# Turning the weights of a three-layer field-interaction kernel: W1 and W0 in one transfer each, V2 spread over interleaved rows, and a new order of TensorE's first products

## The chip, the core and the metric

The kernel runs on one core of one Trainium2 chip. The metric is the device time in microseconds (us). The median of three runs of the kernel before is 738.91 us (738.64 to 738.91).

## The reference, cut to what matters

```python
def _cin_layer(Xk, X0, W, b):                # X0: [B, F, E] = [1024, 39, 64]
    Wr = W.reshape(O, Hk, F)                 # O = H = 64
    return jnp.einsum('bhe,bfe,ohf->boe', Xk, X0, Wr) + b[None, :, None]

Xk = X0
for W, b in ((W0, b0), (W1, b1), (W2, b2)):  # W0: 64 x 39*39, W1 and W2: 64 x 64*39
    Xk = _cin_layer(Xk, X0, W, b)
    outs.append(Xk.sum(axis=-1))
y = jnp.concatenate(outs, axis=-1) @ fc_w.T + fc_b
```

All of it is linear in each weight, so the kernel folds the last layers together. With fc2 the third part of `fc_w`, V2[h, f] is the sum over o of fc2[o] W2[o, h, f]. With V2 (and fc1 as its fortieth column), T[h, f, b] is the sum over o of V2[o, b] W1[o, h, f]. For every sample and every e, the output is then the dot product of two vectors of 64 quadratic forms in the 39 field values: one with the weights W0, one with the weights T plus fc0. Small terms for the biases are added at the end.

## The kernel before, in words

**The main loop.** The 1024 samples times 64 give 65536 columns, taken in 32 blocks of 2048. GpSimd gathers copies of the field rows into tiles `r` (five per block, `gather_rows`, L170; lists of rows in `lists`) and, for each two blocks, `u` and `v`. VectorE multiplies pairs of tiles into products `p` (L211, L213): six chunks of 128 field pairs per block, and one small chunk of 32 rows for each two blocks. TensorE multiplies each `p` with the weights `wa` (L538, L558, L569) into four banks `po`; ScalarE and VectorE finish a block into `sums`. Products are made four steps ahead of TensorE (`AHEAD = 4`).

**The preparation (L216 to L491), where the change lies.** It makes `both`: 64 rows with W0 and 64 rows with T, each with 39 x 40 columns. From `both`, VectorE and ScalarE add the two halves of each field pair into `pairs` (`weight_rows`, L505 and L503), TensorE turns `pairs` (L522), and ScalarE copies it to `wa` (L523, L524). The schedule is written by hand: each engine runs its instructions in the order of the code. The steps on TensorE, with `spin` (L277) a product of constants whose result nobody reads:

1. one `spin` of 512 columns; then `fc_w` turned into columns of the bank `small` (L322, L320), then a `spin` of 512;
2. V2: four products of W2 (`w2s`, 128 rows) with `fc2`, which VectorE makes from `small` (L366), into two banks `pv` (L404). VectorE transposes the banks in 32 x 32 squares (L427), and VectorE and ScalarE copy the columns into two diagonal blocks of `v2` (L437, L438), with fc1 beside them (L434);
3. W0 turned by 20 transposes (L415) from `w0s`, which two transfers have filled on 39 rows each;
4. a `spin` of 512; the biases turned from `brow` (L320, called at L422 and L424); a `spin` of 256;
5. T: four products of W1 (`w1s`, two transfers of 64 rows) with `v2` (L457), copied to `part` (L468), turned by 20 transposes (L477) and copied into `both` (L486). W0 is copied into `both` at L453.
6. two `spin`s of 512, which reach to the first turn of `pairs`.

**The queues.** ScalarE issues the transfers of W2, the first half of the first block's x (`xh[0]`), W0 (two), W1 (two) and `xh[1]`, in this order, before its first computing instruction. SyncE issues `fc_w`, the biases, and then the two copies `xd<-xh` (L394). GpSimd makes small constants (L313, L354 to L358; `pairs` is zeroed at L356), sends a row of ones to DRAM (L361), gathers four `r` from `xh[0]`, loads the second block's x, and gathers four `r` from `xh[1]`, then `r`, `u` and `v` from `xd`.

Of the kernel before, what the change touches and what calls it, by code (L numbers as in the profile page):

```python
# [54 lines left out]
F32 = mybir.dt.float32  # L55
I32 = mybir.dt.int32
AF = mybir.ActivationFunctionType
ALU = mybir.AluOpType
AX = mybir.AxisListType

B, F, E, H = 1024, 39, 64, 64
FH = F * H
FT = F + 1
# [3 lines left out]
NT = 5  # L67
# [7 lines left out]
NCHUNK = NPAIR + 2  # L75
MM = 512
# [3 lines left out]
NQ = NA // 2  # L80
NW = 20
BB = BLK // E
# [4 lines left out]
U_STEPS = ((10, -29), (20, -8), (23, -2), (25, -36), (28, 32))  # L87
V_STEPS = ((0, -3), (20, 6), (25, 33), (28, -35), (31, -39))
# [56 lines left out]
def cin_kernel(ctx: ExitStack, tc: tile.TileContext, x, w0t, b0, w1, b1, w2, b2, fc_w, fc_b, out):  # L145
    nc = tc.nc
# [3 lines left out]
    const = ctx.enter_context(tc.tile_pool(name="const", bufs=1))  # L150
# [6 lines left out]
    xd = [dram.tile([2 * FT, BLK], F32, name=f"xd{k}") for k in range(NTAB)]  # L157
# [17 lines left out]
    def roll(n, tiles=range(NT)):  # L175
        for i in tiles:
            k = n % 2 * NT + i
            gather_rows(rt[n % 2][:, i], xd[n // 2 % NTAB][: FT if k < NT else 2 * FT], k)

    def roll_small(n):  # L180
        table = xd[n // 2 % NTAB].rearrange("f (t c) -> (f t) c", c=SUB)
        for k, dst in enumerate((ut, vt)):
            gather_rows(dst[n // 2 % 2], table, 2 * NT + k)

    wa = const.tile([128, NCHUNK, 3 * H], F32, name="wa")
    columns = const.tile([128, 7], F32, name="columns")
    v2 = const.tile([128, 2, H], F32, name="v2")
    fc0s, b0s = columns[:, 1:2], columns[:, 3:4]
    fcb = const.tile([1, 1], F32, name="fcb")
# [3 lines left out]
    lists = const.tile([128, 2 * NT + 2], I32, name="lists")  # L193
# [23 lines left out]
    with prep as prep:  # L217
        w2s = prep.tile([128, FH // 2], F32, name="w2s")
        w1s = prep.tile([128, FH // 2], F32, name="w1s")
        w0s = prep.tile([128, NW * H], F32, name="w0s")  # L220
        part = prep.tile([FT, 4 * NA, H], F32, name="part")
        fcrow = prep.tile([1, 3 * H], F32, name="fcrow")
        brow = prep.tile([1, 3 * H], F32, name="brow")
        fcrow2 = prep.tile([1, H, 2], F32, name="fcrow2")
        fc2 = prep.tile([128, H], F32, name="fc2")
# [15 lines left out]
        nc.vector.memset(warm, 0.0)  # L241
        w0v = w0t.rearrange("b a h -> b (a h)")
        nc.sync.dma_start(fcrow, fc_w)
        for k, t in enumerate((b0, b1, b2)):
            nc.sync.dma_start(brow[:, k * H : k * H + H], t.rearrange("(o h) -> o h", o=1))
        nc.scalar.dma_start(w2s, w2.rearrange("o (s n) -> (o s) n", s=2))

        def load_half(k):
# [4 lines left out]
        load_half(0)  # L253
        for s, n in enumerate((NW, F - NW)):
            nc.scalar.dma_start(
                w0s[H * s : H * s + F, 0 : n * H], w0v[:, s * NW * H : (s * NW + n) * H]
            )
        for s in range(2):
            nc.scalar.dma_start(
                w1s[H * s : H * s + H], w1[:, s * FH // 2 : (s + 1) * FH // 2]  # L260
            )
        load_half(1)
        nc.gpsimd.iota(place, pattern=[[0, 1]], base=0, channel_multiplier=1)
        nc.gpsimd.iota(apart, pattern=[[1, 128]], base=0, channel_multiplier=-1)
        nc.scalar.copy(warm, warm)


# [7 lines left out]
        def spin(n=1, cols=MM // 2):  # L275
            for _ in range(n):
                nc.tensor.matmul(  # L277
                    idle[:, 0:cols],
                    nc.const_aps.tensor(1.0, (128, 128), F32),
                    nc.const_aps.tensor(1.0, (128, cols), F32),  # L280
                    start=True,
                    stop=True,
                )

        spin(1, MM)

# [23 lines left out]
        for i in range(NT):  # L310
            at = OFFSET[i] - 3 * K + (0 if i < NT - 1 else -F)
            for k, by in enumerate((STEP[i], BASE[i], at)):
                nc.gpsimd.memset(shifts[:, k, i : i + 1], float(by))  # L313
        for s in range(2):
            nc.gpsimd.tensor_copy(fcrow2[:, :, s], fcrow[:, 2 * H : 3 * H])
        one = ones[0:1, 0, 0:1]

        def turn_row(h, at, row, k):
            dst = small[h : h + H, at : at + 1]
            nc.tensor.matmul(dst, row[:, k * H : k * H + H], one, start=True, stop=True)  # L320

        nc.tensor.matmul(  # L322
            small[:, 0:1], fcrow2.rearrange("p h s -> p (h s)"), one, start=True, stop=True
        )
        for k, at in enumerate((1, 2, 4)):
            turn_row(0, at, fcrow, k)
        for k in range(2):
            turn_row(H, k + 1, fcrow, k)
        spin(1, MM)

# [20 lines left out]

        for k, series in enumerate((U_STEPS, V_STEPS)):
            for i, (at, by) in enumerate(series):
                nc.gpsimd.memset(steps_at[:, k, i : i + 1], float(at))  # L354
                nc.gpsimd.memset(steps_by[:, k, i : i + 1], float(by))
        nc.gpsimd.memset(pairs, 0.0)  # L356
        bothv = both.rearrange("p (a b) -> p a b", b=FT)
        nc.gpsimd.memset(bothv[0:H, :, F], 0.0)  # L358

        def fill_ones(k, engine, src):  # L360
            engine.dma_start(xd[k][F::FT].rearrange("r (p c) -> p r c", c=128), src)  # L361

        fill_ones(0, nc.gpsimd, ones)


        nc.vector.tensor_scalar(fc2[:, 0::32], mask, small[:, 0:1], None, ALU.mult)  # L366
        nc.vector.tensor_scalar(unit, apart, 0, None, ALU.is_equal)

# [12 lines left out]
        fused(most, r, 4.0, most, ALU.add, ALU.add)  # L381
        nc.vector.tensor_tensor(seat, seat, far, ALU.add)
        nc.vector.tensor_tensor(both_of[:, 0:1], most, jumps[:, 0:1], ALU.add)
        nc.vector.tensor_tensor(both_of[:, 1:2], both_of[:, 0:1], jumps[:, 1:2], ALU.add)
        nc.vector.tensor_scalar(lists[:, 2 * NT :], both_of, 2.0, seat, ALU.mult, ALU.add)

        halves = [slice(0, SUB), slice(SUB, BLK)]
        for k, cols in enumerate(halves):
            for i in range(4):
                gather_rows(rt[0][:, i, cols], xh[k], i)  # L390
            if not k:
                load(1, nc.gpsimd)
        for k, cols in enumerate(halves):
            nc.sync.dma_start(xd[0][0:F, cols], xh[k])  # L394
        roll(0, (4,))
# [15 lines left out]

        for s in range(2):
            for k in range(NW // 2):
                n = min(128, (F - NW * s) * H - k * 128)
                nc.tensor.transpose(  # L415
                    pw[s][0:n, k * FT : k * FT + F],
                    w0s[H * s : H * s + F, k * 128 : k * 128 + n],
                    unit[H * s : H * s + F, H * s : H * s + F],
                )
        spin(1, MM)  # L420
        for h in (0, H):
            turn_row(h, 3, brow, 0)  # L422
        for k in (1, 2):
            turn_row(0, k + 4, brow, k)  # L424
        spin()
        for k in range(2):
            nc.vector.transpose(  # L427
                blocks[:, k].rearrange("p (f h) -> p f h", h=32),
                pv[k][:, 0:320].rearrange("p (h f) -> p f h", f=10),
            )  # L430
        column = blocks.rearrange("h k (f j) -> h (k f) j", j=32)[:, :, 0]
        for s in range(2):
            rows = slice(H * s, H * s + H)
            nc.scalar.copy(v2[rows, s, F:FT], small[rows, 2:3])  # L434
        for s in range(2):
            rows = slice(H * s, H * s + H)
            nc.vector.tensor_copy(v2[rows, s, 0:20], column[0:H])  # L437
            nc.scalar.copy(v2[rows, s, 20:F], column[H:128, 1:20])  # L438

        roll_small(0)  # L440
        roll(1)
        nc.sync.dma_start(fcb, fc_b.rearrange("(p o) -> p o", o=1))
        fill_ones(2, nc.gpsimd, ones)

# [3 lines left out]

        for k, (a, n) in enumerate(((0, NW), (NW, F - NW))):
            for t in range(2):  # L450
                m = (n + 1 - t) // 2
                src = pw[k][H * t : H * t + H, 0 : m * FT].rearrange("h (a b) -> h a b", b=FT)
                copies[k](bothv[0:H, a + t : a + t + 2 * m - 1 : 2, 0:F], src[:, :, 0:F])  # L453
        w1v = w1s.rearrange("o (h f) -> o h f", f=F)
# [27 lines left out]
        for k, a in groups:  # L482
            for t in range(2):
# [5 lines left out]
                )  # L489
        spin(2, MM)  # L490
        first = [prods.tile([128, BLK], F32, name="p", tag="p") for _ in range(3)]  # L491
# [125 lines left out]
    def last_weights(pk):  # L617

        fc1, fc2, b1c, b2c = (columns[0:H, at : at + 1] for at in (2, 4, 5, 6))
        nc.tensor.matmul(pk[0:F, 0:1], v2[0:H, 0, 0:F], b1c, start=True, stop=True)  # L620
        nc.tensor.matmul(pk[0:1, 1:2], b1c, fc1, start=True, stop=False)
        nc.tensor.matmul(pk[0:1, 1:2], b2c, fc2, start=False, stop=True)
        nc.vector.memset(wfin[0:H], 1.0)
        nc.scalar.copy(wfin[H : H + F], pk[0:F, 0:1])
        nc.scalar.activation(kfin, pk[0:1, 1:2], AF.Identity, bias=fcb, scale=float(E))
# [10 lines left out]
    for k, (n, c) in enumerate(steps[:3]):  # L636
# [12 lines left out]
        else:  # L649
            product(n, c, halves[0], p[n, c])  # L650
    nc.scalar.copy(columns[0:H, 1:7], small[0:H, 1:7])
    nc.scalar.copy(columns[H:128, 1:4], small[H:128, 1:4])
# [114 lines left out]
```

## Time and profile before

| | |
|---|---|
| median of the runs | 738.91 us |
| the profiled execution, and its span from first to last instruction | 738.49 us, 736.7 us |
| TensorE (PE) busy | 732.2 us, 99% of the span |
| VectorE (DVE) busy | 641.0 us, 87% |
| GpSimd (POOL) busy | 386.2 us, 52% |
| ScalarE (ACT) busy | 167.3 us, 23% |
| first main product (L538) starts | 22.10 us after the span's start |

Times below are us after the span's start. "PEld" is TensorE's loading of weights, "SPq", "ACTq" and "PEq" are the engines' own queues of instructions. A product of float32 appears as two records. A busy engine is not an engine at its peak: matmuls are pipelined and their ends are modelled. In the table of groups, a row has the line, the engine, what is written from what, the count, the busy time, the mean duration of one, and the idle time before it with what ended it.

### The profile page before, as it was taken

To read this page: it belongs to the slowest core of one execution; us is meant where nothing else is said; L and a number is where in the kernel's file an instruction comes from. 1 tells how busy PE (TensorE), PEld (TensorE's weight loads), DVE (VectorE), ACT (ScalarE), POOL (GpSimd) and SP (SyncE) were. 2 spreads that over 40 slices of the span, in tenths; PEclk is the share of its full clock that TensorE was granted. 3 is DMA by queue.
4 is the path that set the end of the run, shared out by engine and by line. 5 is a ranking of instruction groups with operands and counts; after the bars stand their busy time and mean duration, and the time that the engine had idled before them with its cause. 6 is when DMAs were issued, how large, how long until landed. Compare 5 with 4: busy or idle time off the path is not lost.

```text
span 736.7 us, 6437 instructions
## 1 busy us (share of the span) xinstructions
PE 732.2 (99%) x2416; PEld 318.0 (43%) x2416; DVE 641.0 (87%) x521; ACT 167.3 (23%) x244; POOL 386.2 (52%) x248
## 2 busy tenths in 40 slices
PE   9999999999999999999999999999999999999998
PEld 5444444444444444444444444444444444444443
DVE  5998899888899888899888899888899888899885
ACT  2332122221212222122221212222122221212222
POOL 6887554457545365554457545365554457545300
PEclk9999999999999999999999999999999999999999
DMA  8989867877576786757878676795767876566700
GB/s 275 376 321 414 300 237 274 347 285 274 227 285 254 286 328 248 282 226 284 334 269 279 244 283 250 287 357 215 282 240 278 328 284 247 217 259 250 285 1 1
DMA packets 65819, 197.25 MB, mean 268 GB/s; under 512 B 39987, under 2 KB 40052, under 8 KB 45819
## 3 DMA queue, kind: packets, MB, share of 16 engines
q0 software_dynamic: 28624, 185.56, 64.8%
q1 hardware_dynamic: 35472, 9.28, 5.5%
q10 hardware_dynamic: 1690, 1.99, 1.0%
q8 instruction: 19, 0.31, 0.2%
q14 instruction: 14, 0.11, 0.0%
HBM read 196.76 MB, written 10.60 MB: 281 GB/s over the span
## 4 chain that ended last, share of the span: by engine, by line
PE 98%; DVE 1%; ACT 0%; issue 0%
PE po L538 90%; PE po L558 4%; PE po L569 2%; PE idle L277 1%; DVE pairs L505 0%; PE pv L404 0%; PE pt L457 0%; DVE p L211 0%; PE pw L415 0%; PE pv L457 0%; PE small L320 0%; PE tr L522 0%; ACT part L468 0%; DVE g L588 0%; DVE sums L610 0%
## 5 line engine op out<-in xcount | busy, mean ns | idle before, releaser
L538 PE MATMUL po<-p,wa 128*128 128x512 f32 x1536 | 665.0, 593 | 0.1
L211 DVE TENSOR_TENSOR p<-r 128x2048 f32<-128x2048 f32 (+2 forms) x197 | 434.1, 2235 | 72.8 <-PE po L538 72.7
L171 POOL DMA_INDIRECT r<-xd,lists x156 | 308.6, 1978 | 286.3 <-issue 277.9
L538 PEld LDWEIGHTS po<-p,wa 128*128 128x128 f32 x1536 | 289.9, 190 | 370.5 <-issue 351.4
L586 ACT ACTIVATE z<-po,columns 64x512 f32<-64x512 f32 x128 | 87.3, 682 | 382.5 <-PE po L569 219.6
L588 DVE SCALAR_TENSOR_TENSOR g<-po,columns,z 64x512 f32<-64x512 f32 x128 | 95.9, 749 | 9.3 <-ACT z L586 5.3
L581 ACT COPY g<-r 39x1024 f32<-39x1024 f32 x64 | 66.7, 1043 | 152.1 <-DVE sums L599 124.9
L599 DVE TENSOR_REDUCE sums<-g 103x16 f32<-103x1024 f32 x62 | 75.6, 1220 | 2.1
L171 POOL DMA_INDIRECT v<-xd,lists x16 | 33.8, 2115 | 4.9 <-issue 4.9
L558 PE MATMUL po<-p,wa 32*64 32x512 f32 x512 | 31.6, 600 | 0.0
L171 POOL DMA_INDIRECT u<-xd,lists x16 | 28.4, 1772 | 4.9 <-issue 4.9
L213 DVE TENSOR_TENSOR p<-u,v 128x1024 f32<-128x1024 f32 x16 | 19.5, 1218 | 0.0
L558 PEld LDWEIGHTS po<-p,wa 32*64 32x64 f32 x512 | 9.4, 131 | 20.2 <-issue 19.4
L569 PE MATMUL po<-u,wa 32*64 32x512 f32 x256 | 17.0, 587 | 0.0
L277 PE MATMUL idle<-const-float32-1.0 128*128 128x512 f32 (+2 forms) x16 | 10.2, 752 | 0.8 <-PEq L754 0.8
L171 POOL DMA_INDIRECT r<-xh,lists x8 | 7.7, 958 | 5.2 <-issue 1.8
L569 PEld LDWEIGHTS po<-u,wa 32*64 32x64 f32 x256 | 5.7, 132 | 8.0 <-issue 8.0
L505 DVE TENSOR_TENSOR pairs<-both 128x2 f32<-128x2 f32 (+27 forms) x59 | 6.1, 171 | 0.4 <-issue 0.3
L523 ACT COPY wa<-tr 128x128 f32<-128x128 f32 x8 | 2.1, 265 | 14.8 <-PE tr L522 14.8
L468 DVE COPY part<-pt 40x320 f32<-40x320 f32 x2 | 1.0, 488 | 4.5 <-PE pt L457 4.5
L277 PEld LDWEIGHTS idle<-const-float32-1.0 128*128 128x128 f32 x16 | 3.4, 252 | 1.4 <-issue 1.2
L165 POOL DMA_DIRECT2D xd<-in_x x3 | 3.2, 1063 | 0.0
(100 smaller groups left out, 61.1 us busy)
## 6 DMA issues: line engine op xcount, KB each, us to landing
xd<-in_x SPq DMA_DIRECT2D x28, 312.0 KB
r<-xd,lists POOLq DMA_INDIRECT x156, 9.1
xd<-in_x POOLq DMA_DIRECT2D x3, 312.0 KB, 8.7
w2s<-in_w ACTq DMA_DIRECT2D x1, 624.0 KB
w1s<-in_w ACTq DMA_DIRECT2D x2, 312.0 KB
xh<-in_x ACTq DMA_DIRECT2D x2, 156.0 KB
xd<-xh SPq DMA_DIRECT2D x2, 156.0 KB
u<-xd,lists POOLq DMA_INDIRECT x16, 9.5
```

Source lines behind the costliest of these rows:

```text
L171: nc.gpsimd.indirect_dma_start(dst, None, table, bass.IndirectOffsetOnAxis(ap=lists[:, k : k + 1], axis=0))
L211: nc.vector.tensor_tensor(p[:, cols], r[:, i, cols], r[:, k, cols], ALU.mult)
L213: nc.vector.tensor_tensor(p[:, 0:SUB], ut[n // 2 % 2], vt[n // 2 % 2], ALU.mult)
L277: nc.tensor.matmul(idle[:, 0:cols], nc.const_aps.tensor(1.0, (128, 128), F32), nc.const_aps.tensor(1.0, (128, cols), F32), start=True, sto ...
L505: nc.vector.tensor_tensor(out, diagonal(a, b, sa, sb), diagonal(b, a, sb, sa), ALU.add)
L538: nc.tensor.matmul(po[n][m], wa[:, c, side : side + 2 * H], p[:, bass.ts(m, MM)], start=n % 2 == 0 and c == 0, stop=n % 2 == 1 and c == NP ...
L558: nc.tensor.matmul(dst[half * H : half * H + H], wa[rows, NPAIR, at : at + H], p[rows, bass.ts(side, MM)], start=t >= 2, stop=t < 2 and ha ...
L569: nc.tensor.matmul(dst[half : half + H], wa[rows, NPAIR + 1, H : 2 * H], ut[n // 2 % 2][rows, bass.ts(side, MM)], start=False, stop=t < 2,)
L581: nc.scalar.copy(gt[H : H + F], rt[n % 2][0:F, 0, bass.ts(m, SUB)])
L586: nc.scalar.activation(z[one], po[n][m][other], AF.Identity, bias=fc0s[other])
L588: return lambda: nc.vector.scalar_tensor_tensor(g[n][m // 2][0:H, at], po[n][m][one], b0s[one], z[one], ALU.add, ALU.mult)
L599: nc.vector.tensor_reduce(sums[:, b_at : b_at + SB], g[n][m // 2].rearrange("p (b e) -> p b e", e=E), AX.X, ALU.add,)
```

## The change

It alters how W0 and W1 lie in SBUF and in which order the preparation runs.

- W1 goes to 128 rows (row 2o + s holds half s of W1's row o) in one transfer; W0 goes to 117 rows (row 3b + s holds a third of row b) in one. `xh[0]` is issued first, W2 next.
- `v2` has a parity pattern in place of two blocks: every row 2o + s holds V2's row o in half s, and zeros in the other. The columns are spread to row pairs by two products with `twice` and multiplied with `mask`. ScalarE no longer writes `v2`.
- W0 needs 7 transposes of 117 x 128 in place of 20 of 39 x 128, and its copies into `both` change engines and pattern.
- TensorE's first `spin`s are 512 + 512 + 256 columns, and the one ahead of V2 128 in place of 512. A `spin` of 256 stands behind V2's products and another behind W0's last three turns. The biases are turned behind T.
- `pairs` is zeroed by ScalarE in place of GpSimd. SyncE's two copies `xd<-xh` change places.

```diff
-NW = 20
+NW = 3
+NF = F // NW
...
-        w0s = prep.tile([128, NW * H], F32, name="w0s")
+        w0s = prep.tile([NW * F, NF * H], F32, name="w0s")
...
-        nc.scalar.dma_start(w2s, w2.rearrange("o (s n) -> (o s) n", s=2))
         load_half(0)
-        for s, n in enumerate((NW, F - NW)):
-            nc.scalar.dma_start(
-                w0s[H * s : H * s + F, 0 : n * H], w0v[:, s * NW * H : (s * NW + n) * H]
-            )
-        for s in range(2):
-            nc.scalar.dma_start(
-                w1s[H * s : H * s + H], w1[:, s * FH // 2 : (s + 1) * FH // 2]
-            )
+        nc.scalar.dma_start(w2s, w2.rearrange("o (s n) -> (o s) n", s=2))
+        nc.scalar.dma_start(w0s, w0t.rearrange("b (s a) h -> (b s) (a h)", s=NW))
+        nc.scalar.dma_start(w1s, w1.rearrange("o (s n) -> (o s) n", s=2))
         load_half(1)
...
+        nc.scalar.copy(
+            pairs.rearrange("p c n -> p (c n)"),
+            nc.const_aps.tensor(0.0, (128, NCHUNK * 128), F32),
+        )
...
-        spin(1, MM)
+        spin(2, MM)
+        spin()
...
+        double(fcrow2, fcrow[:, H : 3 * H])
+        turn_twice(0, fcrow2, 1)
+        turn_twice(6, fcrow2, 0)
+        for h in (0, H):
+            turn_row(h, 1, fcrow, 0)
+        turn_row(0, 4, fcrow, 2)
+        spin(1, MM // 4)
...
-        nc.gpsimd.memset(pairs, 0.0)
...
+        nc.vector.tensor_scalar(unit, apart, 0, None, ALU.is_equal)
+        for h in (0, H):
+            rows = slice(h, h + H)
+            nc.vector.tensor_copy(
+                twice[rows], unit[rows, rows].unsqueeze(2).to_broadcast([H, H, 2])
+            )
         nc.vector.tensor_scalar(fc2[:, 0::32], mask, small[:, 0:1], None, ALU.mult)
+        nc.vector.tensor_scalar(v2[:, :, F], mask, small[:, 6:7], None, ALU.mult)
...
+                double(brow2, brow[:, H : 2 * H])
-        for k, cols in enumerate(halves):
-            nc.sync.dma_start(xd[0][0:F, cols], xh[k])
+        for k in (1, 0):
+            nc.sync.dma_start(xd[0][0:F, halves[k]], xh[k])
...
-        spin(1, MM)
-        for h in (0, H):
-            turn_row(h, 3, brow, 0)
-        for k in (1, 2):
-            turn_row(0, k + 4, brow, k)
         spin()
+        for k in range(4):
+            turn_w0(k)
...
+        for u, (lo, n) in enumerate(((0, 20), (1, 19))):
+            rows = slice(H * u, H * u + H)
+            nc.tensor.matmul(
+                pv[u][:, 0:n],
+                twice[rows].rearrange("p h s -> p (h s)"),
+                column[rows, lo : lo + n],
+                start=True,
+                stop=True,
+            )
+        for k in range(4, 7):
+            turn_w0(k)
+        spin()
+        for u, (lo, n) in enumerate(((0, 20), (20, 19))):
+            nc.vector.tensor_tensor(
+                v2[:, :, lo : lo + n],
+                pv[u][:, 0:n].unsqueeze(1).to_broadcast([128, 2, n]),
+                mask.unsqueeze(2).to_broadcast([128, 2, n]),
+                ALU.mult,
+            )
...
-        spin(2, MM)
+        spin(1, MM)
+        for h in (0, H):
+            turn_row(h, 2, brow, 0)
+        turn_twice(3, brow2, 0)
+        turn_row(0, 5, brow, 2)
+        spin(1, MM)
```

`turn_w0(k)` is one transpose of `w0s[:, 128k : 128k + 128]` into a quarter of a bank `pw`; `turn_twice` turns a row whose elements `double` (two copies on GpSimd) has written twice. Two list computations of VectorE move behind V2, and 20 small memsets of GpSimd ahead of `double`.

## The prediction

> **What bounds the kernel now.** I first asked where TensorE is not the limit. The busy times by stage put that aside for all but the first 42 us: in the last stage (columns: stretch, length, busy PE, PEld, DVE, ACT, POOL, granted clock, share of the DMA engines, GB/s) TensorE works 691.34 of 694.40 us.
>
> ```profile
> 42.30:736.70 694.40, 691.34 (x2275) 298.21 (x2275) 607.39 (x397) 154.11 (x196) 353.09 (x182) 1.00 0.70 264
> ```
>
> The change touches nothing there, so that stage moves as a block. What can change is when the main products begin. The chain that ended last, in order of time (start, us, what), says what sets that:
>
> ```profile
> 4.15 2.01 PE idle L277 x2
> 6.16 2.33 PE pv L404 x8
> 8.49 1.84 PE pw L415 x20
> 10.33 2.00 PE idle L277 x2
> 12.33 0.73 PE small L320 x8
> 13.06 1.15 PE idle L277 x2
> 14.21 2.22 PE pt L457 x4
> 16.43 1.57 PE pv L457 x4
> ...
> 19.61 0.37 DVE both L486
> 19.98 0.28 issue
> 20.27 0.37 DVE pairs L505 x3
> ...
> 25.41 0.30 PE tr L522
> 25.70 7.08 PE po L538 x16
> ```
>
> So the path is the queue of TensorE up to T (18.00), T's copies (to 19.98), VectorE's field pairs and first products (to 25.41), and then the main stream. T cannot start earlier because V2's last parts wait for the biases, which stand behind a dummy; the waits and the gathers' wait read
>
> ```profile
> ACT v L434 <- PE small L320: 3.9, 1, 3.9
> POOL r L171 <- DMA xh<-in_x: 1.7, 1, 1.7
> ```
>
> Last, TensorE's clock. The granted clock is given as 1.00 from the first stage on, but durations (ns min/median/max) of products of 320 columns, by tile, say that it is half until about 17 us:
>
> ```profile
> L404 PE MATMUL pv<-w2s,fc x8: 736/737/792, 6.1 to 7.7; 128*64 128x320 f32 x8
> L457 PE MATMUL pt<-w1s,v x4: 739/740/828, 14.0 to 15.7; 128*128 128x320 f32 x4
> L457 PE MATMUL pv<-w1s,v x4: 451/553/741, 16.2 to 17.5; 128*128 128x320 f32 x4
> ```
>
> **The change, part by part. TensorE at half clock.** T's first four records take 2.22 us for 4 x 320 columns, 1.7 ns a column; the main stream's 16 records take 7.08 us, 0.86 ns a column. The queue ahead of T, in the new order:
> - dummies of 512, 512 and 256 columns, two records each: 2560 x 1.7 = 4.4 us, from 0.78 to 5.2.
> - five turns of fc: 0.58 for the first 128-wide one by L322's row, 0.3 for the second behind it, six records of 0.075 (L320: 0.75 for ten): 1.2, to 6.4. Their source, doubled by GpSimd, is ready before 4 us, so the turns wait only for the dummies.
> - the dummy of 128 columns, 0.5, to 6.9. `fc2` (0.23 on VectorE) hides behind it; bare, it would cost 0.2.
> - V2, 2.33, to 9.25 (before: 8.49).
> - a dummy of 256, 1.1, to 10.35. VectorE's two square transposes (0.52 each) end beside it.
> - seven transposes. The nearest rows are 0.09 (39 x 128) and 0.3 for one alone (L522); I take 0.12: 0.8.
> - two products with `twice`, shown nowhere; four records between 0.3 (L320's rate) and 1.1 (L322's): 0.6.
> - a dummy of 256, 1.1.
>
> All at half clock, T starts at 12.85 in place of 14.21. So the new order gains 1.4 us even if the clock does nothing: out go 20 transposes, the bias turns and a dummy of 2.00, and in come 2.4 us of first dummies, two of 256, and `twice`.
>
> **When the clock is granted.** The Trainium skill (TensorE: Matmul & The Clock Gate, "Part 1: The HAM clock gate") says that full clock comes after one busy window of about 3.4 us, and that the windows run freely. In its short form, 4 us of dense work are enough: then the first dummies do it by 5 us, and all after runs at twice the speed. The rows speak against the short form: from 4.15 to 8.49 TensorE ran a dummy and V2 without a gap, 4.3 us, and the products at 7.7 were still 737 ns. From 13.06 on it ran densely again, and about 4.1 us later the clock was up. Windows of 3.4 us counted back from 17.2 begin at 0.1, 3.5, 6.95, 10.35 and 13.8: the dense stretch of before filled none until the last. If they lie so again, the new dummies (0.78 to 5.2) fill none either, but the dummy of 128, V2 and the dummy of 256 (6.4 to 10.35) fill the third. I take this, full clock from 10.35. What follows then costs 0.5 + 0.4 + 0.55 = 1.45 in place of 2.5, so TensorE is ready at 11.8.
>
> **V2 on VectorE.** It waits for `twice` (about 11.3 with the result's latency), then does an addition or two and two multiplications of about 0.2 (rows of 0.17 to 0.23): V2 stands at 12.0. T starts then: 2.2 us earlier. At full clock it takes 8 x 320 x 0.86 = 2.2 us in place of 3.79: it ends at 14.2, 3.8 earlier.
>
> **T's copies.** W0's copies now stand on VectorE between V2 and T: 585 elements at L453's rate (0.56 for 390) 0.85, and two list operations 0.3, so VectorE is free at 13.15, though T's first bank is there at 12.75. From there it has L468 twice (1.0 each) and L486 four times (0.37): `both` at 16.6, 3.4 us earlier than 19.98. Here 0.4 is given back. ScalarE's half is shorter; its new zeroing of `pairs` (1.0 by L581's copies of 1024) fits in its wait of 3.9.
>
> **The bias turns** now stand between two dummies ahead of the first turn of `pairs`: 0.86 + 0.7 + 0.86 = 2.4 in place of 1.99. TensorE ends T's turns 1.0 ahead of `both` (before 0.6), which hides the 0.4; bare, it costs 0.3, since TensorE had 0.3 us of slack before 25.41.
>
> **Loads.** Neither the 39 nor the 117 rows of W0 use all queues: by the skill (DMA: Bandwidth & Descriptors, "Why a DMA increments its semaphore by 16 and not by 1") the engines of a transfer are the largest number up to 16 that divides its rows: 13 in both cases. No profile row here tells W0's rate, so at the stage's 253 GB/s its 0.39 MB take 1.5 us, by the rule up to 1.9; needed at 10.35, both are covered. W1 is last of 1.83 MB at 253 to 280 GB/s from 1.9 on: 9.6 us, or 10.8 with the gathers' traffic; covered too if T starts at 12.0. The second W0 transfer, which ScalarE could issue only at 5.1, is gone.
>
> **Gathers.** x first, and VectorE's list operation no longer beside the zeroing of `pairs` (1.26 us against some 0.2 of its kind): they start about 1.3 us earlier. The second half's last gather (18.0, landing 6 later) is used by VectorE at 28.6: 4.6 us of slack, more than 3.4. What would be late next are these. SyncE's copies now both wait for the second x half; GpSimd's `r` from `xd` at 19.48 stands behind them and behind eight gathers anyway.
>
> **The sum.** 3.4 us off the profiled execution's 738.49 gives 735.1; the median of the runs is 0.42 above it: 735.5.
>
> **The rivals.**
> - *Clock at once* (0.28). The dummies fill a window, full clock near 5. V2 stands at 9.4, so W1's landing is the new wait, 10.4 (9.6 to 10.8). `both` comes at 14.7, 5.3 earlier; the dummies ahead of the turn of `pairs` give back 0.5: 4.8, time 734.1, at best 733.3. For it: the skill's rule and 4.4 dense us. Against: 4.15 to 8.49 before.
> - *Clock as late as before*, 17.2 (0.20). T starts at 12.85, takes 4.35 at half clock, ends at 17.2: 0.8 earlier, of which the later turn of `pairs` takes up to 0.4: 738.3. For it: V2's window is less than wholly filled if its start slips.
> - *Clock not before the main stream* (0.10), slower. T, earlier by 1.4, ends before the window from 13.8 is full, and the 20 turns and bias turns break the next. The dummies ahead of `pairs` then cost twice 2.0 and the turns 0.7, so the first turn comes at 23.65 in place of 21.30 (2.35 later), and the main stream runs a window at half speed (1.7): 742.9. It decides if no stretch before the main products is dense for a whole window.
> - The forecast: 0.42.
>
> Runs within 0.2% (1.5 us) can't be told from no change. Faster: the first rival, the forecast and a little of the late clock, 0.73; same 0.17; slower 0.10. The range runs from the best of the first rival, 733.3, to just above the late clock, 738.6; it leaves out the slower rival and a little at each end.
>
> **What would show it.** Right: V2's records near 737 ns and W0's turns or T's records near 451; T starting at 12.0; `both` at 16.6; the main stream's first long piece at 22.3 in place of 25.70. The first rival shows V2 near 451 and T waiting for W1. Wrong altogether: VectorE waiting for `r` at its first products, or main products near 1 us each.

## The result, and the profile after

The changed kernel takes 735.99 us in the median of 8 runs (735.12 to 739.1), the kernel before 738.77 beside it: ratio 0.9969, 95% interval 0.9955 to 0.9982. Forecast: 735.5, in a range that holds the result. The profiled execution, the fastest of the eight, took 735.12 us, with a span of 733.3, against 738.49 and 736.7 before.

The chain that ended last, up to the main stream (start, us, what):

```profile
0.77 4.09 PE idle L276 x6
4.87 0.86 PE small L327 x10
...
6.46 1.38 PE pv L411 x8
7.84 0.63 PE idle L276 x2
8.47 0.40 PE pw L423 x4
8.87 0.33 PE pv L439 x4
9.20 0.45 PE pw L423 x3
9.65 0.98 PE idle L276 x2
10.64 0.02 issue
10.66 0.21 DVE v L452
...
10.91 1.43 PE pt L483 x4
12.34 1.18 PE pv L483 x4
...
15.67 0.37 DVE both L512
16.04 0.89 issue
...
21.84 0.30 PE tr L553
```

The main stream's first long piece begins at 22.14 in place of 25.70: 3.56 us earlier, and the execution is 3.37 shorter. Two things differ from the forecast. V2's products (L411) take 1.38, not 2.33: the clock was full already, which is the first rival's sign and not the forecast's. By tile (ns min/median/max, first and last start):

```profile
L411 PE MATMUL pv<-w2s,fc x8: 450/452/502, 6.5 to 7.4; 128*64 128x320 f32 x8
...
L483 PE MATMUL pt<-w1s,v x4: 452/453/553, 10.9 to 11.9; 128*128 128x320 f32 x4
```

And the gain of that clock doesn't arrive whole. There is a piece without work at 16.04, and VectorE's second half of V2 starts 1.39 after the first (9.27), though its product (L439) ends at 9.20. The waits of the first 23 us name both places (in total, times, longest; "seen late" below means such a wait behind a product whose record has ended):

```profile
PEld pt L483 <- DVE v L452: 1.2, 1, 1.2
ACT both L512 <- issue: 1.2, 1, 1.2
DVE v L452 <- PE idle L276: 1.2, 1, 1.2
```

T doesn't wait for W1, and no first product waits for `r`.

### The profile page after: what moved, and what is told of

It reads as the page before. It is cut to its first block, busy times and chain, and to the rows that moved or that the text cites. A ratio compares the mean times of both kernels' runs of the same rounds, so it can differ in the third digit from the quotient of the medians.

```text
span 733.3 us, 6426 instructions
## 1 busy us (share of the span) xinstructions
PE 727.3 (99%) x2409; PEld 316.4 (43%) x2409; DVE 640.9 (87%) x524; ACT 168.7 (23%) x241; POOL 384.7 (52%) x249
## 3 DMA queue, kind: packets, MB, share of 16 engines
q1 hardware_dynamic: 35472, 9.28, 5.5%
q10 hardware_dynamic: 1700, 1.99, 0.9%
## 4 chain that ended last, share of the span: by engine, by line
PE 98%; DVE 1%; issue 0%; ACT 0%
PE po L569 90%; PE po L589 4%; PE po L600 2%; PE idle L276 1%; DVE pairs L536 0%; DVE p L212 0%; PE pt L483 0%; PE pv L411 0%; DVE both L512 0%; PE pv L483 0%; PE tr L553 0%; PE small L327 0%; PE pw L423 0%; DVE g L619 0%; DVE sums L641 0%
## 5 line engine op out<-in xcount | busy, mean ns | idle before, releaser
L172 POOL DMA_INDIRECT v<-xd,lists x16 | 31.8, 1989 | 4.9 <-issue 4.9
L553 PE MATMUL tr<-unit,pairs 128*128 128x128 f32 x8 | 2.3, 283 | 0.6 <-ACT wa L555 0.5
```

Of the source, the lines that this page charges most:

```text
L172: nc.gpsimd.indirect_dma_start(dst, None, table, bass.IndirectOffsetOnAxis(ap=lists[:, k : k + 1], axis=0))
```

## Fourteen executions side by side

Each kernel below left one profiled execution. "Clock" is the moment from which the trace's record gives the full TensorE clock for good; "main" is the first main product behind the third turn of `pairs`; T runs from its first to its last record; `both` is the end of the later engine's copies.

| kernel | clock | T | `both` | main | time | time - main |
|---|---|---|---|---|---|---|
| before | 17.19 | 14.00-17.99 | 20.18 | 25.54 | 738.49 | 712.95 |
| after | 4.21 | 10.91-13.50 | 16.89 | 21.98 | 735.12 | 713.14 |
| again | 15.60, also 5.36-8.78 | 13.70-17.05 | 19.24 | 24.73 | 738.26 | 713.53 |
| again_b | 16.63 | 14.40-17.90 | 21.06 | 26.71 | 739.64 | 712.93 |
| short_dummies | 13.91 | 13.86-16.37 | 18.56 | 24.05 | 737.02 | 712.97 |
| dummies_alone | 9.71 | 13.94-16.53 | 20.58 | 25.98 | 738.91 | 712.93 |
| biases_alone | 16.07 | 13.02-16.90 | 20.16 | 25.50 | 738.43 | 712.93 |
| both_moves | 4.25, lost 21.32-24.73 | 11.35-13.91 | 19.10 | 25.52 | 738.24 | 712.72 |
| turns_20 | 9.89 | 13.31-15.79 | 18.37 | 23.92 | 736.87 | 712.95 |
| w0_by_field | 16.48 | 13.82-17.52 | 19.71 | 25.20 | 738.12 | 712.92 |
| no_dummy_behind | 4.16-7.57, 10.99-17.82, from 21.23 | 12.37-14.96 | 17.73 | 23.90 | 736.82 | 712.92 |
| x_behind | 4.49 | 9.68-12.16 | 14.69 | 20.25 | 734.00 | 713.75 |
| x_behind_b | 10.14 | 12.13-14.63 | 18.65 | 23.74 | 736.88 | 713.14 |
| best | 4.96 | 10.28-12.76 | 16.08 | 21.16 | 734.29 | 713.13 |

The last column is nearly constant, so the prediction's first step stands: all that counts is when the main stream begins. The rest of this section and the experiments are about what sets that. The four kernels no_dummy_behind, x_behind, w0_by_field and turns_20 ran on another chip, where the kernel before has a median of 735.6 (one group of runs near 735.2, one near 738.2), so their ratios compare only with each other. The changed kernel itself did not run there.

## The experiments

The theory after the result: the gain is the earlier main stream; the clock's moment decides how early; late sight of finished products ate part. The rivals: the dense dummies alone, the moved biases alone, the earlier loads, or the fewer turns are the whole gain.

**again**: the changed kernel, unaltered.

> The changed kernel once more, nothing altered. Theory A (the gain is mostly TensorE's clock being up early, and the moment at which it comes differs from run to run): the median is again near 736.0, single runs lie between 735 and 739, and this profile may show another moment than 4.2 us, with V2's products (L411) near 450 ns or near 737 ns accordingly. Theory B (the gain is the new order, the clock hardly matters): the same median, but a spread as narrow as before's (1 us). In both, the second half of V2 (L452) is looked at: in the first profile it began at 10.66, 1.4 us behind the first half, though TensorE's records of its product end near 9.2.

Ratio 0.9969 (0.9957 to 0.9981). Same kernel, another clock: granted at 5.36, lost at 8.78, back at 15.60. The table by stage (length, PE, PEld, DVE, ACT, POOL busy, clock, DMA share, GB/s) shows why it fell: in the window before, TensorE was busy for 2.08 of 3.42 us. It stood idle there for 1.34 us ahead of V2, which began at 8.00; x_behind below says why this was a wait for W2.

```profile
5.36:8.78 3.42, 2.08 (x19) 1.64 (x20) 1.39 (x12) 1.35 (x3) 2.55 (x3) 1.00 0.98 273
8.78:12.19 3.41, 3.41 (x16) 1.86 (x11) 1.14 (x4) 0.45 (x1) 2.36 (x4) 0.50 1.05 396
```

**short_dummies**: `spin(2, MM)` and `spin()` at the start become `spin(1, MM)`.

> The changed kernel with the first dummies of before: one of 512 columns in place of 512 + 512 + 256. Theory A: V2's products run at half clock (near 737 ns), T starts about 1 to 2 us later than in the changed kernel's profile (10.91), and the time is 1 to 2 us longer, 737 to 738. Theory B: the time stays at 736.0 or is a little shorter, since 2 us of dummies in front of V2 are gone.

0.9974 (0.9966 to 0.9982): not told apart from the changed kernel. The clock came at 13.91. V2 began at 7.53, 1.67 after TensorE was free, so it was not the dummies that held it (it waited for W2, see x_behind).

**dummies_alone** and **biases_alone**, on the old kernel:

```diff
-        spin(1, MM)
+        spin(2, MM)
+        spin()
```

```diff
-        for h in (0, H):
-            turn_row(h, 3, brow, 0)
-        for k in (1, 2):
-            turn_row(0, k + 4, brow, k)
...
-        spin(2, MM)
+        spin(1, MM)
+        for h in (0, H):
+            turn_row(h, 3, brow, 0)
+        for k in (1, 2):
+            turn_row(0, k + 4, brow, k)
+        spin(1, MM)
```

> The kernel before with only the first dummies of the change (512 + 512 + 256 columns in place of 512). Theory A: V2 near 450 ns, T at full clock and starting at about 12 (W1 lands then) in place of 14.21; the time 735.5 to 736.5. Theory B: no gain, 738.8, or up to 1 us longer because V2 stands behind 2.4 us more of dummies.

> The kernel before with only the turns of the biases moved behind T (between the two dummies there); the dummies keep their sizes. Theory A: V2 is ready near 9.6 but TensorE's dummies end at 13.4 at half clock, so T starts 0.8 us earlier at most; 738.0 to 738.8. Theory B: the wait for the biases was the limit, and most of the gain is here: 736 to 737.

0.9998 (0.9984 to 1.0012) and 0.9988 (0.9980 to 0.9997). The dummies did bring the clock early (9.71), but T still started at 13.94, for V2's last columns, which wait for the bias turns, stood at 13.89. With the bias turns moved V2 stood at 9.58 and T started at 13.02, at half clock. The rows of dummies_alone, then of biases_alone:

```profile
13.44 0.45 ACT L439 COPY v<-blocks 64x19 f32<-64x19 f32 x2
...
13.94 1.43 PE L458 MATMUL pt<-w1s,v 128*128 128x320 f32 x4 [0.24 <-ACT v L439]
```

```profile
13.02 2.34 PE L453 MATMUL pt<-w1s,v 128*128 128x320 f32 x4
```

**both_moves**: the two together.

> The old kernel with two parts of the change together: the dense first dummies (512, 512 and 256 columns) and the bias turns moved behind T. Alone, the first brought nothing (0.9998) and the second 0.5 us (0.9988). Nothing else: 20 turns of W0, V2 copied as before, loads as before. Theory: each was worthless alone because T waited for V2's last columns (13.9) when the clock came early, and the clock was late when V2 came early; together T starts near 12 at full clock and the kernel gains 1.5 to 2.5 us over the old one, ratio 0.9970 to 0.9980, most of the whole change. Rival: the two only add, 0.9985 or above, and the rest of the gain comes from the new layout (7 turns in place of 20, V2 in products, W0 and W1 in one transfer each).

0.9982 (0.9961 to 1.0002): unclear. The mechanism expected is there: clock at 4.25, T at 11.35 (it waited 0.71 for W1, in its two transfers). But 3.0 us went behind T. Timeline rows (start, length, engine, line; in brackets the idle time before):

```profile
14.48 1.00 PE L474 MATMUL pt<-unit,part 40*128 40x40 f32 x10
...
15.41 1.13 PE L277 MATMUL idle<-const-float32-1.0 128*128 128x512 f32 x2
...
16.90 1.13 PE L277 MATMUL idle<-const-float32-1.0 128*128 128x512 f32 x2
18.48 0.62 ACT L483 COPY both<-pt 64x160 f32<-64x160 f32 x2 [2.88 <-issue]
```

The last turns are over at 15.48, and ScalarE copies them at 18.48, when both dummies are through. TensorE then stood idle, and the clock was lost for a window at 21.32.

**no_dummy_behind**: the `spin()` behind W0's last turns and the `spin(1, MM)` behind T's turns taken out.

> The changed kernel without two of its dummies: the 256-column one behind W0's last turns and the 512-column one behind T's turns. Theory: the end of a product that stands ahead of a long dummy is seen by the other engines only when that dummy is through; that cost the changed kernel 1.2 us ahead of V2's second half and 0.9 us ahead of the last copy of T. Then the gap between V2's two halves on VectorE falls from 1.39 us (start to start) to about 0.2, ScalarE's last T copies start within 0.4 us of the end of the turns (before 0.9), and the time falls by 0.5 to 1.0, to 735.0 to 735.5. Rival 1: the delay has nothing to do with the dummies; then the gaps stay and the time is 736.0. Rival 2: the dummies keep TensorE's clock up, and without them it comes a window later: 737 to 738, with T's records above 700 ns.

0.9992 (0.9973 to 1.0011) on the other chip. The late sight was gone in its profile (V2's halves 0.12 apart, ScalarE's last copies within 0.1 of the turns' end), and so was the steady clock: it fell at 7.57 and 17.82. Times lay between 733.25 and 739.24, and no gain is to be seen. The fall at 17.82 fits the second rival: it comes right behind the place where the dummy behind T's turns is missing (T's turns end at 17.05). The fall at 7.57 does not, since both dummies that were taken out stand behind that moment; there TensorE waited 1.72 us for W2 (see x_behind). That the dummies cause the late sight is not shown: turns_20 has the same dummy there and ScalarE is not late:

```profile
16.88 0.81 PE L503 MATMUL pt<-unit,part 40*128 40x40 f32 x10
...
17.62 1.13 PE L276 MATMUL idle<-const-float32-1.0 128*128 128x512 f32 x2
...
17.73 0.62 ACT L512 COPY both<-pt 64x160 f32<-64x160 f32 x2 [0.31 <-PE pt L503]
```

**x_behind**, and **x_behind_b** beside the changed kernel **again_b**: the line `load_half(0)` goes behind W2's transfer.

> The changed kernel with W2's transfer issued before x's first half, as it was before; nothing else. Theory: x first only moves the gathers (4.96 in the changed kernel, 6.5 in the old one), which have some 4 us of slack where VectorE first needs the second half: 736.0, within 0.5, the gathers' start about 1 us later. Rival: the earlier gathers are part of the 2.8 us, because the second half's last gather would else be late: 737 or more, with VectorE or GpSimd waiting for r in the first products.

> The changed kernel once more, unaltered, as the base of the runs beside it. In the kernels profiled so far the time follows the start of the main stream's long piece, which follows the moment at which the full clock is granted, and that moment differs between executions of one kernel (4.2, and 5.4 with a loss until 15.6). Theory: the times spread over some 4 us with a median 1 to 2.5 below the kernel before, ratio 0.9970 to 0.9985.

> The changed kernel with W2's transfer ahead of x's first half, again, now beside the changed kernel on one chip. Theory: x first brings nothing, and W2 earlier lets V2's products begin with the end of the dummies instead of 0.3 to 1 later: 0 to 1.0 us faster than the changed kernel. Rival: equal within 0.3.

On the other chip 0.9976 (0.9964 to 0.9988); beside each other 0.9974 (0.9961 to 0.9987) for x_behind_b and 0.9974 (0.9963 to 0.9984) for the changed kernel. The ratios show no difference between the orders, to within about 1 us. The spread is another: seven of x_behind_b's 22 runs lie between 733.72 and 734.66, where none of the eight of again_b is (735.86 at best).

What the order does in the trace is plain. With x first, W2 lands later (its last landing event is at 4.84 in x_behind, but at 6.57, 7.06 and 7.69 in turns_20, w0_by_field and no_dummy_behind), and V2's products can wait for it. First no_dummy_behind (x first), then x_behind (W2 first):

```profile
7.83 2.40 PE L411 MATMUL pv<-w2s,fc 128*64 128x320 f32 x8 [1.72 <-DMA w2s<-in_w]
```

```profile
6.20 1.38 PE L411 MATMUL pv<-w2s,fc 128*64 128x320 f32 x8
```

TensorE stood idle ahead of V2 for 1.72 in no_dummy_behind, 1.67 in short_dummies, 1.34 in again, 0.51 in again_b and 0.32 in the changed kernel's first profile, not at all in turns_20 and w0_by_field, and never in the seven executions with W2 first. (Where the rows name VectorE for this wait, `fc2` had been ready for 0.4 us or more: at 6.53 in again, while W2's landing events go on to 7.25 at least.) The two early losses of the clock, at 8.78 in again and at 7.57 in no_dummy_behind, end the windows in which the waits of 1.34 and 1.72 began.

The single execution of x_behind shows both sides of it. Its clock was full at 4.49, nothing was seen late, V2 stood at 9.28 and `both` at 14.69, 2.2 us ahead of the changed kernel's profile. But its gathers start at 6.81 (4.96 with x first), and its chain now runs through them (start, us, what):

```profile
13.17 1.00 POOL r L172
14.47 7.27 DMA r<-xh,lists
21.84 1.24 DVE p L212
23.21 4.53 PE po L569 x10
```

The main stream stops for 0.8 until the last gather has landed (713.75 in the table). So the gathers are next late, once `both` comes before 15. x first doesn't always help: in again and again_b the second half of x landed late, GpSimd waited 6.5 us for it, and its gathers began at 17.7 in place of 11.35 (in again that cost 0.6).

**w0_by_field**: W0 is turned against an identity whose columns are taken by residue (every third column, three times), so that its copies run along 39 elements.

```diff
-                unit[0 : NW * F, 0 : NW * F],
+                unit[0 : NW * F, 0 : NW * F].rearrange("p (b s) -> p s b", s=NW),
```

> The changed kernel with W0 turned against an identity whose columns are taken in another order, so that the turned rows come out by residue of the field, and its copies move runs of 39 in place of single elements with a step. Theory: the dearer W0 copies (1.39 us on VectorE for 585 elements, 2.00 on ScalarE for 936, against 0.56 for 390 in the old kernel) are the price of the pattern of 3; in runs they take 0.85 and 1.35, VectorE comes to T's copies 0.5 us earlier, and `both` and the time fall by up to 0.5: 735.5. Rival: VectorE waits for T at that point or the last wait of `both` is ScalarE's, and it changes nothing: 736.0 with shorter copies. Second rival: the copies keep their length, so the pattern isn't what they cost.

0.9985 (0.9971 to 0.9999) on the other chip: no gain to be seen. The copies did shrink. First the changed kernel, by tile:

```profile
L468 ACT COPY both<-pw x2: 990/996/1001, 9.2 to 10.2; 64x468 f32<-64x468 f32 x2
L468 DVE COPY both<-pw x2: 586/686/785, 10.8 to 11.6; 64x351 f32<-64x351 f32 x1, 64x234 f32<-64x234 f32 x1
```

Then w0_by_field:

```profile
L468 ACT COPY both<-pw x2: 542/544/545, 11.9 to 12.4; 64x468 f32<-64x468 f32 x2
L468 DVE COPY both<-pw x2: 403/460/516, 13.2 to 13.7; 64x351 f32<-64x351 f32 x1, 64x234 f32<-64x234 f32 x1
```

So the pattern is the price (in the changed kernel W0's copies write single elements, in turn to three places 520 elements apart): 0.92 against 1.37 on VectorE, 1.09 against 1.99 on ScalarE. In this execution the clock came at 16.48, T's first bank was late, and VectorE waited for it 0.68 us. How much time the shorter copies save with an early clock is not shown.

**turns_20**: 20 turns of W0 in place of 7, some repeated.

```diff
-        for k in range(4):
+        for k in (0, 1, 2, 0, 1, 2, 3, 0, 1, 2, 3):
...
-        for k in range(4, 7):
+        for k in (4, 5, 6) * 3:
```

> The changed kernel with 20 turns of W0 in place of 7, as many as before (the same seven, some of them repeated into the same places). Theory: the turns ahead of T stand on the path, so 13 more at 0.075 to 0.15 each make T 1.0 to 2.0 later: 737.0 to 738.0, which would make the turns the largest single part of the gain. Rival: V2's path over VectorE hides them, at least the first half of them beside VectorE's square transposes (1.1 us): 736.0 to 736.5.

1.0010 (0.9996 to 1.0023) on the other chip, against 0.9976 and 0.9985 of its neighbours there: 1.8 to 2.5 us are gone, and with that all of the gain. With the clock at nearly the same moment (9.89 and 10.14) T starts at 13.31 here and at 12.13 in x_behind_b, so 1.2 us of it are seen directly. First turns_20, then x_behind_b:

```profile
11.90 1.12 PE L423 MATMUL pw<-unit,w0s 117*128 117x117 f32 x9
...
13.31 1.32 PE L483 MATMUL pt<-w1s,v 128*128 128x320 f32 x4
```

```profile
11.33 0.52 PE L423 MATMUL pw<-unit,w0s 117*128 117x117 f32 x3
...
12.13 1.34 PE L483 MATMUL pt<-w1s,v 128*128 128x320 f32 x4
```

The turns stand on the path. But this run does not put the old turns back: the thirteen that it adds have 117 columns each, the twenty of the kernel before had 39. At half clock those twenty took 1.84 us (8.49 in the chain before), and the seven new ones take 1.56, as the chain of w0_by_field has them:

```profile
11.04 0.78 PE pw L423 x4
...
12.37 0.78 PE pw L423 x3
```

So fewer turns save about 0.3 us of TensorE's time (an estimate from these rows), not the 2 us of this run.

**best**: w0_by_field's edit, W2 ahead of x, and VectorE's W0 copies behind its copies of T (T's turns then go to `pt`).

> The changed kernel with three edits: W2's transfer ahead of x, W0 turned by residue so that its copies run along 39 elements, and VectorE's half of W0's copies moved behind its copies of T (T's turns then go into the four banks that T itself filled). Theory: VectorE is at T's first bank as soon as it is full, so `both` comes 0.5 to 1.0 us earlier and the time is 0.7 to 1.5 us below the changed kernel's beside it. Rival: with the clock late TensorE is the bound up to `both` and VectorE waits anyway; then no more than the gain of W2 first, 0 to 0.5.

0.9965 (0.9953 to 0.9977) beside 0.9974 (0.9963 to 0.9984) of the changed kernel. It beats the kernel before; over the changed kernel the gain is not shown. VectorE took T's first bank when it came, but ScalarE saw the last turns 0.85 late.

## Why the prediction was right, and where it was not

**The block and the sum.** Right: time follows the start of the main stream to within 0.3 us, but for two executions with late gathers.

**The clock.** This step failed as it was put: full clock from 4.21 in the profile, not from 10.35. Windows of 3.41 to 3.42 us are what the records show (5.36 to 8.78; 4.16 to 7.57; 17.82 to 21.23), as the Trainium skill says (TensorE: Matmul & The Clock Gate, "Part 1: The HAM clock gate"), and it says too that they run freely. I laid them back from one trace, took that phase for the kernel's, and made the other moments rivals. They are outcomes of one kernel: three executions of the changed kernel had full clock from 4.21, 15.60 and 16.63. The phase explains the early ones. The dummies run from 0.78 to 5.38 at half clock, so they fill a whole window if it begins between 0.78 and 1.97, and the grant then falls between 4.19 and 5.38. Six of the eleven executions with dense dummies have it there, or within 0.03: 4.16, 4.21, 4.25, 4.49, 4.96 and 5.36. If the phase is even, 1.19 of 3.41, or 35%, would be expected (an estimate). Otherwise it came near 10, as forecast (9.71, 9.89, 10.14), when a dummy and V2 filled a window, and in the other two executions at 16.48 and 16.63.

The page gives an idle window as what takes the clock back; here 2.08 busy of 3.42 lost it, 2.60 of 3.41 kept it (after, 7.62 to 11.03), and in no_dummy_behind 2.93 of 3.42, mostly turns of 40 columns, lost it. In dummies_alone 1.66 of 3.42 kept it (19.95 to 23.37). So the busy time of the records doesn't tell which window loses the clock; what does stays open.

**The queue at half clock** was 1 us too short. In w0_by_field, at half clock until T has begun, T starts at 13.82, not 12.85. The terms that were too small: the dummies take 4.6 (forecast 4.4), fc's turns 1.45 (1.2), and the seven turns 1.56 (0.8), because I took the rate of turns of 39 columns for turns of 117. Of the 1.4 us that I gave the new order without any clock, 0.2 to 0.4 are left (the old kernel's T starts at 14.00 by its first record, 14.21 in its chain), and in again_b, where V2 waited for W2, nothing (14.40).

**V2** at 12.0: it stood at 10.86 in the profile, with the full clock from 4.21, and 1.2 of that was late sight. Of the first rival's numbers, V2 at 9.4 and `both` at 14.7, x_behind has 9.28 and 14.69, and its time was 734.0 where 734.1 was forecast; it is a single execution, of a kernel with W2 first. The rival's new wait, W1's landing, didn't come: T started at 9.68. (My 9.6 for that landing doesn't follow from its figures, which give 8.4 to 9.1; in the four executions with W1 in one transfer whose trace has all of its landing events the last is at 9.39, 9.39, 9.80 and 10.64.) The wait that came was for the gathers, the step that I had named as next late.

**T's copies.** W0's copies were mis-sized: 1.39 us in place of 0.85, since I took the rate of rows of 39. `both` was complete at 16.89, against 16.6. "ScalarE's half is shorter" didn't hold: ScalarE ended 0.85 after VectorE (16.04), as it saw the last turns late.

**The sum** came out right because these cancel: a clock a window or two earlier than forecast in this execution, two late sights of 1.2 and 0.9, dearer copies. For this execution that is luck. The median, 735.99, lies between its time and those of the two later profiles of the changed kernel (738.26 and 739.64), about where the middle case was put. None of the three lies within 0.8 us of the median, so what an execution near it does is not shown.

**Hidden steps.** The bias turns cost nothing: from `both` to main it is 5.36 before and 5.1 to 5.65 in the kernels with the turns there, but for the two that lost the clock in between (6.2 in no_dummy_behind, 6.4 in both_moves). ScalarE's zeroing of `pairs` (1.04 at 5.71) fits. The gathers started 1.67 earlier. One step I put at nothing without a reason: W2, moved behind x. It cost 0.32 to 1.72 us ahead of V2 in five of the seven executions with x first, and the clock in two of them. No whole median showed the slower rival; single executions did end slower (again_b, 739.64).

**Which part gives the gain?** That is not settled. The one part that gains alone is the move of the bias turns (0.0012 of 738.5, 0.9; between the medians 0.5). The dummies alone give nothing, and the changed kernel with only one of its first dummies (short_dummies) is not told apart from the whole. Fewer turns save about 0.3 of TensorE's time at half clock. V2's new spread and the single transfers were not tried alone, so most of the 2.8 us is not assigned to a part. What the table does show, with different kernels and one execution of each, is that with the new layout the main stream starts later the later the clock comes: at 20.25 to 21.98 in the three with full clock by 5 for good (after, x_behind, best), at 23.74 to 24.05 in the three where it came between 9.9 and 13.9 (x_behind_b, turns_20, short_dummies), and at 24.73, 25.20 and 26.71 in the three where it came for good after 15. In no_dummy_behind, whose clock comes and goes, it is 23.90. The old kernel, with the clock at 17.19, has 25.54.

## What to carry to other kernels

In these executions the moment of TensorE's full clock near the start was largely a draw of the window's phase: 4.6 us of dense work held a whole window of 3.41 us in six of eleven. So forecast such a moment as a mixture, and profile a kernel more than once before explaining one execution. Look also for what leaves TensorE idle inside a window: here a reordered load did. Price a turn by what it streams: seven turns of 117 columns cost nearly what twenty of 39 did (1.56 against 1.84). Dummies brought nothing alone (0.9998), since the next consumer was waiting for something else. When two waits stand in parallel, test them together: each alone may show nothing.

## What was not expected of the hardware

In seven of the thirteen profiles with a 512-column dummy behind T's turns, an engine began to copy finished turns 0.8 to 3.0 us late, each within 0.5 us of the end of a dummy behind them (after, again_b, x_behind_b, both_moves, best, dummies_alone, biases_alone); in the other six, the kernel before among them, within about 0.3. The same kernel showed both (again in time, again_b late). Without that dummy the one profile has no such wait.

The trace's semaphore events (the signals by which TensorE tells the others that a product is done) add one thing. In the changed kernel's first profile the signals of V2's second product, of W0's last turns and of the dummy behind them come together, at 10.64, 10.69 and 10.73, though their records end at 9.20, 9.65 and 10.10. In x_behind the same three come at 8.99, 9.41 and 9.86, within 0.05 of the records' ends. So the dummy's own signal is late too. Since the ends of the records are modelled, this can't tell signals that were held back from a TensorE that stood still. Whether the dummy causes it, and what draws the two cases, stays open.

A copy that wrote single elements, in turn to three places 520 elements apart, took 2.1 ns an element on ScalarE and 2.3 on VectorE; with runs of 39 it took 1.2 and 1.6.
